# Layer 3 of a four-layer convolution chain: GpSimd's side work paced by an account of its own, and the next heads' keys and values fetched one block earlier

## The chip, the cores and the metric

The kernel runs on one core of one Trainium2 chip. The metric is the device time of one execution in microseconds (us), lower is better; before the change it is 3645.99 us, the median of three runs (3644.94 to 3652.72). The core has five engines that matter here, each working through its own queue in order: TensorE (PE, with weight loads shown as PEld), VectorE (DVE), ScalarE (ACT), GpSimd (POOL) and SyncE (SP), which here issues nearly all DMAs.

## The reference, cut to what matters

Four layers follow each other, each `x = x + layer(groupnorm(x))` on `x` of shape (4, 256, 48, 48). Layers 0 to 2 are convolutions, and the change does not touch them. Layer 3 is an attention with box windows of three sizes (48, 24 and 12 rows and columns) and 8 heads of 32 channels:

```python
q, k = sigmoid(Wq x), sigmoid(Wk x)              # per head: 32 channels x 48 x 48
v = v / max(norm(v), 1e-12)
for w in (1, 2, 4):                              # window of 48/w x 48/w positions
    wk, wkv = box(k), box(k v^T)                 # sums over the window around each position
    attn = (q . wkv) / (q . wk + 1e-6)           # numerator / "norm"
out = Wout concat(attn of the 3 windows) + bout
```

## The kernel before, in words

**The stream.** The kernel does not build `k v^T` images. For each block it computes scores `s = k^T q` between 128 key positions and 384 query positions, multiplies them by 0/1 window masks into tiles `sm`, and multiplies `sm` by `v` into three accumulators `acc`, one for each window. A block is (batch b, half of the heads ct, band of 8 rows rb): 4 x 2 x 6 = 48 blocks, numbered 0 to 47 in this order. A block has 12 to 18 steps, one for each tile of 8 x 16 key positions; the list `stream` (L2106) has 720 steps in all. The loop at L2143 does, for step n: the scores of step n on TensorE, the masks of step n, and then the sums (`acc`) of step n - 2 (`LAG = 2`). VectorE and ScalarE take the masks out of PSUM; GpSimd makes the mask of the narrowest window from an `sm` tile that VectorE or ScalarE has written (`masked`, L1809). In the trace these are the POOL operations `sm<-sm,masks`. So TensorE needs GpSimd's product of step n just before its scores of step n + 3.

**Everything else is put between the steps.** All instructions keep the order in which the Python code issues them (class `InOrder`; this is why nearly every line of the profile reads L147, and why groups are told apart by their tiles). Side work is written as generators, "jobs", and `advance()` (L241) lets each job issue its next piece after every step. The jobs are

- the projections of the next batch to q, k, v (`Projection`, L425: `sq`, the squares of v, on GpSimd; a VectorE sum and a ScalarE root follow);
- `k_sums` (L1559): running sums of k down the image, eight GpSimd additions on `pt` for each band, in two portions of four, then a store to `kb_d`;
- `norms` (L1601): loads `nhi`, `nlo`, `nq`, up to twelve GpSimd operations on `nhi` in four portions of three, a TensorE product, and the reciprocal by way of DRAM (`n_d`, `r_d`);
- `state` and `window_state` (L1700, L1730): for the part of the widest window in which every query sees every key, products of keys and values, then small GpSimd additions `kv` and `wide`;
- `prepare` (L1957): loads the first half's results `o` and the reciprocals `rc`, and multiplies them on GpSimd, three operations;
- `finish` (L1990): the output projection `out_ps`, two chains of six products.

**The account of TensorE.** `advance(time)` gives `spare`, the room that TensorE is expected to have in this step; a job that wants TensorE waits in `turn` (L268) or `bank` (L275) until `spare` is at least 0.6 of its cost, and takes the cost off. There is no account of GpSimd: a portion goes out at the step at which its job gets there.

**Forced steps.** Where the stream cannot go on without a job's result, `until(...)` (L257) calls `advance()` with unlimited room again and again, with no step of the stream in between. It is called for `("done", i - 2)`, since the sums of block i reuse the buffers of block i - 2, for `("window", i)` before the wide part of block i, and for q, k and v before they are loaded.

**Keys and values** of the next half of the heads are loaded by `load_kv` (L1686) at the end of the blocks that the table `LOADS` (L2059) names by their band, and each load starts a `state` job.

Of the kernel before, what the change touches and what calls it, by code (L numbers as in the profile page):

```python
# [22 lines left out]
B, C, H, W = 4, 256, 48, 48  # L23
# [3 lines left out]
RB = 8  # L27
NRB = H // RB
NB = RB * W
# [45 lines left out]
HEADS, D = 8, 32  # L75
# [75 lines left out]
def conv_preact_kernel(  # L151
# [82 lines left out]

    step, bank_free, spare = 0, 0, 0.0
    made = set()
    active = []

    def advance(time=None):  # L241

        nonlocal step, spare
        step += 1
        spare = ALL if time is None else min(spare, 0.0) + time
        for entry in list(active):
            if entry[0] <= step:
                wait = next(entry[1], None)
                if wait is None:
                    active.remove(entry)  # L250
                else:
                    entry[0] = step + wait
# [10 lines left out]
        while not made.issuperset(keys):  # L263
            yield 1

    ALL = 1e6

    def turn(cost):  # L268

        nonlocal spare  # L270
        while spare < 0.6 * cost:
            yield 1
        spare -= cost

# [22 lines left out]
    def take(what):  # L297
        while free[what] == 0:
            yield 1
        free[what] -= 1  # L300
# [11 lines left out]
    class Projection:  # L312
# [84 lines left out]
        def v(self, g, a, c):  # L397
            b = self.b
            while g not in self.xn or (c > 0 and g not in self.vs):
                if g in self.left:  # L400
                    return
                yield 1
            if c == 0:
                yield from take("vt")
                self.vs[g] = (
                    self.scr.tile([P, NKC, HEADS, D], F32, tag="vt", name="vt"),
                    self.scr.tile([P, NKC, HEADS], F32, tag="ss", name="ss"),
                )
            vt, ss = self.vs[g]
            yield from bank(1, NCT * product_time(C))  # L410
            ps = self.ps_tile()[:, 0:C].rearrange("p (h d) -> p h d", d=D)
            for ct in range(NCT):
                pe.matmul(
                    ps,
                    self.xn[g][:, ct, c, :],
                    proj["v"][:, ct, :],
                    start=(ct == 0),
                    stop=(ct == NCT - 1),
                )
            self.used(g)  # L420
            yield 1
            act.copy(vt[:, c], ps)
            yield 1
            yield from take("sq")
            sq = self.scr.tile([P, HEADS, D], F32, tag="sq", name="sq")  # L425
            pool.tensor_mul(sq, vt[:, c], vt[:, c])
            yield 2
            dve.tensor_reduce(ss[:, c, :], sq, AX.X, ALU.add)
            free["sq"] += 1
            if c < NKC - 1:  # L430
                return

            n = NKC * HEADS
            t = ss.rearrange("p k h -> p (k h)")
            r, s, u = (small.tile([P, n], F32, tag=f"{x}{n}", name=x) for x in ("vr", "vs", "vu"))
            dve.tensor_scalar_max(t, t, 1e-24)
            yield 1
            act.activation(s, t, AF.Sqrt)
            yield 1
            dve.reciprocal(r, s)  # L440
            dve.tensor_mul(u, t, r)
            dve.tensor_mul(u, u, r)
            dve.tensor_scalar(u, u, -0.5, 1.5, ALU.mult, ALU.add)
            dve.tensor_mul(r, r, u)
            dve.tensor_mul(
                vt,
                vt,
                r.rearrange("p (k h) -> p k h", h=HEADS)
                .unsqueeze(3)
                .to_broadcast([P, NKC, HEADS, D]),  # L450
            )
            yield 1
            sync.dma_start(out=v_d[b][:, a * NKC : (a + 1) * NKC], in_=vt)
            free["vt"] += 1
            made.add(("v", b, a))
# [1051 lines left out]
    with (  # L1507
# [51 lines left out]
        def k_sums(b, a, mo):  # L1559

            yield from wait_for(("k", b, mo, a))
            kp = kps[mo]
            chans = slice(mo * P, (mo + 1) * P)
            sync.dma_start(
                out=shifted(kp, 0),
                in_=kf_d[b][chans, a * NB : (a + 1) * NB].rearrange("p (r x) -> p r x", x=W),
            )
            yield FETCH
            yield from take("cs")
            cs = scr.tile([P, (RB + 1) * ROW], F32, tag="cs", name="cs", bufs=1)  # L1570
            n = GAP + RB * ROW
            for i, j in ((0, n // 2), (n // 2, n)):
                dve.tensor_tensor_scan(
                    cs[:, i:j],
                    kp[:, i:j],
                    kp[:, 0:1].to_broadcast([P, j - i]),
                    cs[:, i - 1 : i] if i > 0 else 0.0,
                    ALU.add,
                    ALU.add,
                )  # L1580
                yield 1
            pt = scr.tile([P, NW, RB, W], F32, tag="pt", name="pt")
            for wi, h in enumerate(HALVES):
                dve.tensor_sub(pt[:, wi], shifted(cs, h - 1), shifted(cs, -h - 1))
                yield 1
            free["cs"] += 1
            for r in range(RB):
                if a > 0 or r > 0:
                    up = pt[:, :, r - 1, :] if r > 0 else carry[:, mo]
                    pool.tensor_add(pt[:, :, r, :], pt[:, :, r, :], up)  # L1590
                if r == RB // 2 - 1:
                    yield 1
            pool.tensor_copy(carry[:, mo], pt[:, :, RB - 1, :])
            yield 1
            sync.dma_start(
                out=kb_d[b][:, chans, a * RB : (a + 1) * RB, :].rearrange("w p r x -> p w (r x)"),
                in_=pt.rearrange("p w r x -> p w (r x)"),
            )
            made.add(("kb", b, mo, a))

        def norms(b, rb):  # L1601
# [41 lines left out]
            for hi, lo, qf in loaded:  # L1643
                for wi, h in enumerate(HALVES):
                    n = min(RB, max(0, h + 1 - rb * RB))
                    if n < RB:
                        pool.tensor_sub(hi[:, wi, n:RB], hi[:, wi, n:RB], lo[:, wi, n:RB])
                yield 1
                for wi in range(NW):
                    pool.tensor_mul(hi[:, wi], hi[:, wi], qf)  # L1650
                sums.append(hi)
                yield 1
            yield 1
            yield from bank(HOLD, 2 * product_time(NB))
            ps = ps_m.tile([P, 512], F32, tag="st", name="norm_ps")
# [74 lines left out]
        def window_state(i):  # L1730


            b, ct, rb = order[i]
            rows = [a for a in range(NRB) if rows_whole(a, rb)]
            yield from wait_for(*(("state", b, ct, a) for a in rows))
            st = states[b, ct]
            t = scr.tile([P, NKC, D], F32, tag="kv", name="kv")
            pool.tensor_add(t, st[:, rows[0]], st[:, rows[1]])
            for a in rows[2:-1]:
                pool.tensor_add(t, t, st[:, a])  # L1740
            yield 1
            for g in range(HG):
                head = slice(g * D, (g + 1) * D)
                pool.tensor_add(wides[i % 2][head, :, head], t[head], st[head, rows[-1]])
            made.add(("window", i))
# [193 lines left out]
        def seen(wi, a, rb):  # L1939
            r0, r1 = rows_seen(wi, a, rb)  # L1940
            return r0 < r1
# [15 lines left out]
        def prepare(i):  # L1957
# [24 lines left out]

            yield FETCH
            for wi in range(NW):
                pool.tensor_mul(o[:, wi], o[:, wi], rcs[0][:, wi])
                yield 2
            free["rc"] += 1
            prepared[i] = o, res, rcs[1]

# [66 lines left out]
            load_kv(0, 0, a)  # L2056


        LOADS = {2: (0,), 3: (1, 2), 4: (3, 4), 5: (5,)}  # L2059
        finishing = []  # L2060

        def finish_all():
# [48 lines left out]
        def mask_time(i, a, c):  # L2111
# [11 lines left out]
                return time + product(1, cols_seen(1, c))  # L2123
            return time + 300

        def sums_time(i, a, c, at):

            rb, time = order[i][2], 0
            for wi in range(NW):
                if seen(wi, a, rb):  # L2130
                    y0, y1 = rows_seen(wi, a, rb)
                    parts = strips(c) if wi == 0 and rows_whole(a, rb) else [cols_seen(wi, c)]
                    time += product_time((y1 - y0) * sum(p1 - p0 for p0, p1 in parts))
            if at == 0:
                time += 300
            if at == 6:
                time += product_time(sum(RB * (c1 - c0) for c0, c1 in map(cols_whole, range(NKC))))
            return time
# [4 lines left out]
        for n in range(len(stream) + LAG):  # L2143
# [8 lines left out]
            if n >= LAG:  # L2152
# [11 lines left out]
                        blocks[i].sums(wi, a, c, sms)  # L2164
                if last:
                    done(i)
            time = 1000.0
            if LAG <= n < len(stream):
                time = 150.0 + mask_time(*stream[n][:3]) - sums_time(*stream[n - LAG][:4])
            advance(max(time, 150.0))  # L2170
        while active:
            advance()

# [43 lines left out]
```

## Time and profile before

| | |
|---|---|
| median of three runs | 3645.99 us (3644.94 to 3652.72) |
| the profiled execution, its own time | 3656.03 us |
| its span in the trace | 3654.3 us |
| layers 0 to 2, up to the first scores | 1396 us |
| layer 3's stream, to the end | 2258 us |
| TensorE busy in the stream | 2015 us |
| GpSimd busy in the stream | 1513 us |
| VectorE, ScalarE busy in the stream | 1484 us, 401 us |

The profile page slices the span in 40 equal parts of 91 us; the stream is roughly parts 16 to 40. A row of waits names the waiting engine and tile, the one that ended the wait, the sum in us, how often, and the longest. A line of the timeline has the start in us, the duration, engine and line, the operation with its tiles and how many were merged, and in brackets the idle time of the engine just before and what ended it.

### The profile page before, as it was taken

The numbers are of one execution on the slowest core, as the hardware profiler recorded it, in microseconds if no ns is written. First come the engines' busy times: TensorE is split into PE (matmuls) and PEld (weight loads), VectorE is DVE, ScalarE is ACT, GpSimd is POOL, SyncE is SP. The second block draws the span as 40 slices with busy tenths as digits, with TensorE's granted clock in tenths as the row PEclk, the third lists the DMA queues.
The fourth block names the chain that finished last, engine by engine and source line by source line (L and its number), as shares of the span: only waits on it lengthen the run. The fifth ranks groups of instructions, "written<-read, shape, count | busy, mean of one in ns | idle before, by whom it ended". The sixth has DMA issues, their size and how long they took to land. (4 is left out here: it accounts for less than half of the span.)

```text
span 3654.3 us, 73033 instructions
## 1 busy us (share of the span) xinstructions
PE 3184.0 (87%) x28754; PEld 1921.4 (53%) x28754; DVE 2408.1 (66%) x4987; ACT 677.1 (19%) x1557; POOL 1668.1 (46%) x2548
## 2 busy tenths in 40 slices
PE   3589998998998787888889888899898999899998
PEld 2467686786776564444444444444444444444444
DVE  7876587488474356687756567766567766566665
ACT  0012111111213522221101132211123211111110
POOL 0000020030030125697876577877557876555554
PEclk9789999999999898999889999999999999999999
DMA  7746324323313513353634343434323434311221
GB/s 251 228 140 189 114 82 129 109 91 116 124 51 119 164 68 97 103 156 121 180 98 121 98 137 123 127 124 143 87 72 121 147 111 137 84 40 37 69 70 51
DMA packets 373031, 422.76 MB, mean 116 GB/s; under 512 B 129075, under 2 KB 328531, under 8 KB 371667
## 3 DMA queue, kind: packets, MB, share of 16 engines
q1 hardware_dynamic: 371491, 416.32, 36.7%
q8 instruction: 229, 3.75, 0.4%
q0 software_dynamic: 144, 0.99, 0.1%
q14 instruction: 111, 0.91, 0.1%
q10 hardware_dynamic: 1056, 0.79, 0.1%
HBM read 287.74 MB, written 131.25 MB: 115 GB/s over the span
## 5 line engine op out<-in xcount | busy, mean ns | idle before, releaser
L147 DVE TENSOR_TENSOR sm<-s,masks 128x128 f32<-128x128 f32 (+8 forms) x2592 | 1146.4, 496 | 716.9 <-PE s L147 305.6
L147 POOL TENSOR_TENSOR sm<-sm,masks 128x432 f32<-128x432 f32 (+14 forms) x1152 | 824.1, 728 | 688.7 <-DVE sm L147 513.6
L147 PE MATMUL s<-qs,ks 32*128 32x320 f32 (+3 forms) x5760 | 819.4, 511 | 109.0 <-DVE sm L147 55.8
L147 PE MATMUL acc<-sm,vs 128*32 128x64 f32 (+13 forms) x14976 | 689.9, 310 | 49.0 <-POOL sm L147 48.2
L147 PE MATMUL cv<-vx,wt 128*128 128x288 f32 x2080 | 562.5, 427 | 93.1 <-DVE vx L147 50.7
L147 PEld LDWEIGHTS acc<-sm,vs 128*32 128x32 f32 x14976 | 354.2, 112 | 466.2 <-issue 273.0
L147 PEld LDWEIGHTS s<-qs,ks 32*128 32x128 f32 x5760 | 329.5, 190 | 487.7 <-issue 204.5
L147 PEld LDWEIGHTS cv<-vx,wt 128*128 128x128 f32 x2080 | 404.3, 199 | 215.3 <-issue 55.1
L147 POOL MEMSET v<- 128x16 f32 (+1 forms) x120 | 18.5, 215 | 727.8 <-DVE vx L147 633.6
L147 ACT COPY sm<-s 128x234 f32<-128x234 f32 (+5 forms) x384 | 124.5, 342 | 868.1 <-PE s L147 720.5
L147 PE MATMUL cv<-v,wl 128*128 128x384 f32 x1152 | 225.2, 356 | 24.3 <-DVE x L147 9.1
L147 PEld LDWEIGHTS cv<-v,wl 128*128 128x128 f32 x1152 | 215.7, 196 | 33.9 <-issue 15.8
L147 POOL TENSOR_TENSOR pt<-pt 128x144 f32<-128x144 f32 x336 | 189.8, 565 | 23.8 <-DVE pt L147 1.0
L147 POOL TENSOR_TENSOR v<-l2v,v 128x384 fp32r<-128x384 f32 x96 | 108.9, 1163 | 130.2 <-ACT v L147 121.5
L147 POOL TENSOR_TENSOR nhi<-nhi,nq 128x384 f32<-128x384 f32 x144 | 144.7, 1032 | 0.1
L147 PE MATMUL cv<-pad,wl 128*128 128x384 bf16 x864 | 143.1, 328 | 0.0
L147 PE MATMUL out_ps<-o,wout_sb 128*128 128x384 f32 x288 | 134.1, 548 | 4.2 <-DVE res L147 3.4
L147 ACT COPY stage<-acc 128x384 f32<-128x384 f32 x144 | 64.0, 488 | 365.3 <-PE acc L147 345.6
L147 PE MATMUL out_ps<-stage,wout_sb 128*128 128x384 f32 x288 | 120.4, 501 | 0.0
L147 PE MATMUL proj_ps<-xn,wk_sb 128*128 128x384 f32 x192 | 89.8, 596 | 31.3 <-ACT sg L147 24.6
L147 DVE TENSOR_TENSOR vx<-v 128x868 f32<-128x868 f32 x112 | 115.3, 1055 | 0.5
L147 PEld LDWEIGHTS <-wl 128*128 128x128 bf16 x864 | 83.9, 97 | 59.4 <-issue 0.8
(174 smaller groups left out, 3320.0 us busy)
## 6 DMA issues: line engine op xcount, KB each, us to landing
wt<-wt SPq DMA_DIRECT2D x48, 768.0 KB
kb_d<-pt SPq DMA_DIRECT2D x48, 576.0 KB
rc<-r_d SPq DMA_DIRECT2D x192, 144.0 KB
nhi<-kb_d SPq DMA_DIRECT2D x120, 192.0 KB
nlo<-kb_d SPq DMA_DIRECT2D x88, 192.0 KB
o_d<-stage SPq DMA_DIRECT2D x24, 576.0 KB
o<-o_d SPq DMA_DIRECT2D x24, 576.0 KB
wl<-wl_d SPq DMA_DIRECT2D x16, 768.0 KB
```

The source lines that it names most:

```text
L147: return lambda *args, **kwargs: self.tc.keep_in_program_order(op(*args, **kwargs))
```

## The change

GpSimd gets an account like TensorE's. `advance` gives `slack` as well, 1000 ns and the expected time of the step's masks less GpSimd's own mask time; `pool_turn` holds a job back until `slack` is at least 0.3 of the cost of its next GpSimd operations, and takes the cost off. Marked `urgent`, it only takes the cost off. `k_sums` now goes by two additions at a time, `norms` and `prepare` by one operation at a time, and the fixed pauses between their portions go. TensorE's threshold in `turn` becomes 0.3 too, and that of `bank` stays 0.6. Every entry of `LOADS` moves to the band before.

```diff
-    def advance(time=None):
+    def advance(time=ALL, pool_time=ALL):
         step += 1
-        spare = ALL if time is None else min(spare, 0.0) + time
+        spare = min(spare, 0.0) + time
+        slack = min(slack, 0.0) + pool_time
...
+    def pool_turn(elements, times=1, urgent=False):
+        nonlocal slack
+        cost = times * pool_op(elements)
+        while slack < 0.3 * cost and not urgent:
+            yield 1
+        slack -= cost
+
+    def pool_op(elements):
+        return 190 + 1.95 * elements
+
     def turn(cost):
-        while spare < 0.6 * cost:
+        while spare < 0.3 * cost:
...
             yield from take("sq")
+            yield from pool_turn(C, urgent=True)
...
             for r in range(RB):                                   # k_sums
+                if r % 2 == 0:
+                    if r > 0:
+                        yield 1
+                    yield from pool_turn(NW * W, 2)
                 if a > 0 or r > 0:
                     up = pt[:, :, r - 1, :] if r > 0 else carry[:, mo]
                     pool.tensor_add(pt[:, :, r, :], pt[:, :, r, :], up)
-                if r == RB // 2 - 1:
-                    yield 1
...
                     if n < RB:                                    # norms
+                        yield from pool_turn((RB - n) * W)
                         pool.tensor_sub(hi[:, wi, n:RB], hi[:, wi, n:RB], lo[:, wi, n:RB])
-                yield 1
-                for wi in range(NW):
+                    yield from pool_turn(NB)
                     pool.tensor_mul(hi[:, wi], hi[:, wi], qf)
                 sums.append(hi)
-                yield 1
...
+            yield from pool_turn(NKC * D, 2, urgent=True)         # window_state
             t = scr.tile([P, NKC, D], F32, tag="kv", name="kv")
...
-            yield 1
             for g in range(HG):
+                if g % 2 == 0:
+                    yield 1
+                    yield from pool_turn(NKC * D, 2, urgent=True)
...
             for wi in range(NW):                                  # prepare
+                yield from pool_turn(NB)
                 pool.tensor_mul(o[:, wi], o[:, wi], rcs[0][:, wi])
-                yield 2
+                yield 1
...
-        LOADS = {2: (0,), 3: (1, 2), 4: (3, 4), 5: (5,)}
+        LOADS = {1: (0,), 2: (1, 2), 3: (3, 4), 4: (5,)}
...
+        def far_time(i, a, c):
+            rb = order[i][2]
+            wi = NW - 1 if seen(NW - 1, a, rb) else 1
+            if not seen(wi, a, rb):
+                return 0
+            (y0, y1), (x0, x1) = rows_seen(wi, a, rb), cols_seen(wi, c)
+            return 2 * pool_op(2 * (y1 - y0) * (x1 - x0))
...
-            time = 1000.0
+            time, pool_time = 1000.0, 1000.0
             if LAG <= n < len(stream):
-                time = 150.0 + mask_time(*stream[n][:3]) - sums_time(*stream[n - LAG][:4])
-            advance(max(time, 150.0))
+                masks_ = mask_time(*stream[n][:3])
+                time = 150.0 + masks_ - sums_time(*stream[n - LAG][:4])
+                pool_time = 1000.0 + masks_ - far_time(*stream[n][:3])
+            advance(max(time, 150.0), max(pool_time, 150.0))
```

More of the change, by code (lines that the diff above doesn't have):

```diff
@@ L232, in conv_preact_kernel @@
     proj = {}
-    step, bank_free, spare = 0, 0, 0.0
+    ALL = 1e6
+    step, bank_free, spare, slack = 0, 0, 0.0, 0.0
     made = set()
     active = []
-    def advance(time=None):
-        nonlocal step, spare
+    def advance(time=ALL, pool_time=ALL):
+        nonlocal step, spare, slack
         step += 1
-        spare = ALL if time is None else min(spare, 0.0) + time
+        spare = min(spare, 0.0) + time
+        slack = min(slack, 0.0) + pool_time
         for entry in list(active):
@@ L264, in wait_for @@
             yield 1
-    ALL = 1e6
+    def pool_turn(elements, times=1, urgent=False):
[6 more added lines that the diff above has]
+        return 190 + 1.95 * elements
     def turn(cost):
         nonlocal spare
-        while spare < 0.6 * cost:
+        while spare < 0.3 * cost:
             yield 1
```

## The prediction

> **What bounds the kernel now.** I read the page's slices first, for where GpSimd is loaded, then busy time by stretches of the stream (the columns are stretch, length, then busy us and count of PE, PEld, DVE, ACT and POOL, then clock, DMA share and GB/s), then TensorE's waits from 1396 us on.
>
> ```profile
> POOL 0000020030030125697876577877557876555554
> 1721.00:2010.00 289.00, 257.09 (x2858) 122.92 (x2856) 188.82 (x399) 34.74 (x102) 220.77 (x317) 0.93 0.46 133
> 3393.00:3654.30 261.30, 242.13 (x2825) 118.48 (x2825) 160.00 (x354) 26.54 (x78) 130.58 (x193) 0.99 0.22 66
> PE acc L147 <- POOL sm L147: 48.2, 44, 4.9
> PE acc L147 <- POOL wide L147: 14.2, 3, 7.1
> PE norm_ps L147 <- ACT sg L147: 9.0, 1, 9.0
> ```
>
> TensorE is busy for 2015 of the stream's 2258 us, so its gaps, 243 us, are all that a new order of the same instructions can save. The last stretch, with almost no side work, has 19 us of gaps in 261; the second has 32 in 289, with GpSimd at 76%. TensorE waits 62.4 us on GpSimd itself. The timeline shows how:
>
> ```profile
> 1820.30 3.21 POOL L147 TENSOR_TENSOR nhi<-nhi,nq 128x384 f32<-128x384 f32 x3
> 1823.47 1.79 POOL L147 TENSOR_TENSOR sm<-sm,masks 128x312 f32<-128x312 f32 x2
> 1824.59 0.46 PE L147 MATMUL acc<-sm,vs 128*32 128x156 f32 x4 [2.90 <-POOL sm L147]
> ```
>
> Three `nhi` stand in GpSimd's queue ahead of a mask, the mask is late, and the sums wait 2.90 us. The lateness also goes round by other queues:
>
> ```profile
> 1697.86 2.62 POOL L147 TENSOR_TENSOR pt<-pt 128x144 f32<-128x144 f32 x4
> 1700.51 0.37 SPq L147 DMA_DIRECT2D kb_d<-pt  x1
> 1701.81 1.35 SPq L147 DMA_DIRECT2D q_d<-sg  x2
> 1705.68 1.28 ACT L147 ACT_TABLE_LOAD   x1 [7.49 <-DMA q_d<-sg]
> 1707.52 1.50 PE L147 MATMUL norm_ps<-nhi,head_sel 128*32 128x384 f32 x6 [8.97 <-ACT sg L147]
> ```
>
> `pt` is late, SP's store of it holds back the stores of `sg` behind it, ScalarE waits for those to reuse the buffer, and TensorE waits 8.97 us for ScalarE.
>
> **What the Trainium skill says.** "Perfetto Trace Analysis", Optimization Strategy, says to look for the gaps of the contended engine and for the semaphore that ends each; that is the method here, and its warning in Identifying the Most-Contended Engine that matmul busy time hides pipelining is why I count gaps and not the 89%. "GPSIMD Engine Reference", Elementwise, gives about 2.6 cycles an element at 1.2 GHz for two inputs, an estimate of 832 ns for 384 elements ahead of dispatch; the page's row for `nhi` has 1032 ns, and I use that. "DMA: Bandwidth & Descriptors", Anatomy of one DMA, says that a semaphore is waited for on the issuing sequencer before dispatch; the 1700.51 and 1701.81 lines agree.
>
> **Part 1, the bursts that go.** No instruction is added or removed on any engine; only the order changes. I counted in the built order what side work each step puts into GpSimd's queue, at the page's means (`pt` 565 ns, `nhi` 1032 ns; `o` 1011, `sq` 652 from the groups). Before, 30 of 720 steps put in over 4 us, against a mean step of 3.1 us; after, 11, and ten of these are forced stretches. So the paced part does what it says. Its account has room: the formula allows 299 us per batch, the side work is about 250. The TensorE waits for `sm` in blocks whose bursts are broken up sum, from the timeline, to 33.4 us: blocks 3 and 4 1.7, block 5 2.4, 7 5.8, 8 8.2, 15 5.5, 17 to 19 6.0, 30 and 31 3.8. I take three quarters, 25 us, because the account forgets unspent room and new small clusters appear (steps 457 to 462). The roundabout wait, 9.0 us, goes too. If the smoothed queue were still late by the same amount, this part would be worth nothing.
>
> **Part 2, `LOADS` one band earlier.** Both forced stretches on windows 24 and 36 (steps 368 and 548) go from the order, with one wait each:
>
> ```profile
> 3181.26 2.18 PE L147 MATMUL acc<-qs,wide 128*128 128x192 f32 x5 [3.58 <-POOL wide L147]
> ```
>
> That is 7.2 us. The third `wide` wait, 7.1 us at step 8, stays: it is the first block's. The earlier loads are part of the same 96 DMAs, a block sooner in SP's queue; the buffers hold two halves, so no load waits for one, and no stretch is forced on k or v.
>
> **Part 3, a load that leaves ScalarE's way.** At step 182 ScalarE waited for a batch-1 input queued on SP behind a dozen norm loads, with TensorE behind it:
>
> ```profile
> 2032.24 1.30 ACT L147 ACTIVATE xn<-xr,st 128x384 f32<-128x384 f32 x2 [14.44 <-DMA xr<-x_d]
> 2033.97 1.70 PE L147 MATMUL s<-qs,ks 32*128 32x320 f32 x8 [6.80 <-ACT sm L147]
> ```
>
> After, those loads are issued earlier and `xn` comes outside the stretch: 6.8 us gained. The four items make 25 + 9.0 + 7.2 + 6.8 = 48 us.
>
> **Part 4, the forced stretches, which grow.** Pacing delays `k_sums`, these delay `norms`, `norms` delays `prepare` and `finish`; so finished blocks are asked for too early more often. After the first block the order has 33 forced advances before and 50 after: new stretches at steps 137 (eight), 350 and 530 (five each), longer ones at 170 and 299. In a forced advance the room is unlimited, so `pool_turn` never yields and the twelve `nhi` that were four portions come out as one. What a burst costs is seen at step 542:
>
> ```profile
> 3153.39 2.93 POOL L147 TENSOR_TENSOR nhi<-nhi,nlo 128x384 f32<-128x384 f32 x3
> 3166.77 1.76 POOL L147 TENSOR_TENSOR sm<-sm,masks 128x168 f32<-128x168 f32 x3
> 3167.34 0.96 PE L147 MATMUL acc<-sm,vs 128*32 128x84 f32 x10 [4.85 <-POOL sm L147]
> ```
>
> Its scores end at 3151.07. The burst of twelve `nhi` and two `o` delays the mask to 15.7 us after that. TensorE is covered for 11.4 us, by three pairs of `out_ps` (1.3 us each), the sums in hand and three steps; the rest is the wait. I price each stretch so. At 350 and 530 the norm loads are issued inside the stretch, and GpSimd waits for them in its queue. At step 182 before, such a wait ended 6.6 us after the end of the scores (2017.19):
>
> ```profile
> 2016.98 0.33 SPq L147 DMA_DIRECT2D r_d<-nr  x1
> 2023.83 1.01 POOL L147 TENSOR_TENSOR nhi<-nhi,nlo 128x384 f32<-128x384 f32 x1 [4.14 <-DMA nlo<-kb_d]
> ```
>
> So 6.6 + 13.4 of work (3153.39 to 3166.77 above) = 20.0, less 11.4 of cover: 8.6 us each, 17.2. At 137: eight `pt` and `carry` fill the time until the loads land at 7.5, then twelve `nhi`, three `o`, four `pt` to 24.7; five pairs of `out_ps` cover 15: 9.7, less the 2.6 us that block 9 loses now, 7.1. At 299: ten `nhi`, three `o`, cover 10: 4.2. At 362 and 542 a third `o` and the single burst make 5.9 each, against 1.7 and 4.85 now: 5.3. At 182: 2.9. At 170 and 194: 1.4 against 5.4 now, a gain of 4.0. The sum is 33 us lost. Not seen in any trace of before is a stretch with sixteen loads and 22 us of side work at once; from below it costs 0 (loads landed, cover as long as the burst), from above 20 us at 137 and 18 at each of 350 and 530 (no cover but `out_ps`), 30 us more than I take.
>
> **Part 5, edits costed at nothing.** `turn` at 0.3 lets a chain's later products start in tighter steps; TensorE's work is the same, and the cover is that it is the busy engine anyway; if two products then crowd one step, VectorE idles for one product, about 1.3 us. `bank`'s threshold is unchanged, and so are the 40 us of waits of `proj_ps` on ScalarE's `sg` and `vt`, within 10 us either way. Four of the last block's products move from the tail into the last steps, where gaps are small: 0 to 1 us.
>
> **Sum.** 3656.0 - 48 + 33 = 3641 against the profiled execution's own time. That execution lies 10 us above the median, so the forecast for the median is **3631 us**, 0.4% faster. A measurement of this kernel can tell about 0.2%, 7 us, from no change.
>
> **Rivals.** *Forced stretches decide* (0.23, slower): the mechanism is the single burst of Part 4, its place steps 137, 350 and 530, its price up to 18 to 20 us each. Against the gain of 48 it decides once the stretches cost over 55 us together; at 33 + 30, with half of the 25 us, it gives 3646 + 63 - 35 = 3674. For it speaks that these stretches are new and carry more than any before; against it, that the 14 us burst at 542 cost just 4.85. *The smoothing is hidden anyway* (0.17, no change): TensorE's waits for GpSimd turn into waits on VectorE's or ScalarE's masks, which already sum to 102 us, so that only Parts 2 and 3 remain; with half of Part 4's loss that is about 3648. *More follows than I count* (0.10): smoother `sq` and `pt` also shorten the `proj_ps` waits, by half of 40 us, and the loads in the stretches land early: 3600. That the change does not do what it says is excluded by the order for GpSimd, except in forced stretches.
>
> **From cases to numbers.** The likeliest case (0.5) has 3631, its own range 3617 to 3645. The range of 3602 to 3664 reaches into the slower and the better case and leaves out about 2 in 10. Faster by over 0.2%: 0.43 from the first case, 0.10 from the last, 0.01 else: 0.54. Within: 0.07 + 0.14 + 0.02 = 0.23. Slower: 0.23.
>
> **What would show it.** Right: TensorE's wait for `wide` falls from 14.2 to 7 us; the 9 us of `norm_ps` on `sg` and the 6.8 us near step 182 are gone; no wait for `sm` over 2 us in blocks 5 to 8; new ones of about 9 us after steps 137, 350 and 530, behind a run of twelve `nhi`. Wrong: waits for `sm` as large as 48 us outside forced stretches, or over 15 us behind each of the three.

## The result, and the profile after

The changed kernel takes 3653.54 us (median of 22 runs, 3639.23 to 3668.93), against 3652.01 us (22 runs, 3640.86 to 3660.14) for the kernel before on the same chips. The ratio is 1.001, with a 95% interval of 0.9998 to 1.0021: no change that can be measured. The forecast had been 0.4% faster. Single runs scatter (standard deviation 6 to 7 us), so the experiments are read by their ratios to the kernel before, whose intervals are narrower, and "us under the changed kernel" below is the difference of two such ratios times 3652; such a difference is uncertain by 6 to 11 us.

The page of the changed kernel shows the same shape of GpSimd's load as before:

```profile
POOL 0000030030030124688986577776556687645554
```

The first slices of the stream are a little lower (`4688986` where `5697876` stood), the later ones are hardly different. So the account spreads the load over a few steps, not over a batch. Two stretches, with the columns of the prediction's windows:

```profile
1690.00:1981.00 291.00, 253.38 (x2866) 123.67 (x2865) 203.01 (x417) 35.06 (x103) 236.52 (x342) 0.95 0.45 131
3392.00:3648.80 256.80, 239.66 (x2820) 117.55 (x2816) 158.54 (x356) 24.57 (x69) 131.67 (x193) 1.00 0.23 67
```

In the quiet last stretch TensorE's gaps are 17 us of 257 (19 of 261 before). In the busy one, where the change was to help, they are 38 of 291, against 32 of 289. TensorE's waits from the first scores (1391 us) on, the largest rows:

```profile
PE s L147 <- DVE sm L147: 63.2, 151, 3.5
PE s L147 <- ACT sm L147: 50.7, 94, 5.9
PE proj_ps L147 <- ACT sg L147: 47.0, 22, 5.7
PE acc L147 <- POOL sm L147: 27.9, 15, 6.0
PE proj_ps L147 <- ACT vt L147: 19.6, 21, 1.7
PE out_ps L147 <- DVE res L147: 9.7, 5, 2.5
PE acc L147 <- POOL wide L147: 6.1, 1, 6.1
```

The sums wait for GpSimd's `sm` 15 times instead of 44, and for 27.9 us instead of 48.2; `wide` falls from three waits to one; the 9 us wait of `norm_ps` is gone. What the prediction counted on did happen. But the projections, `proj_ps`, now wait 66.6 us for ScalarE's `sg` and `vt`, and waited 39.7 before. The rows of the kernel before:

```profile
PE s L147 <- DVE sm L147: 55.8, 153, 2.9
PE s L147 <- ACT sm L147: 46.0, 90, 6.8
PE proj_ps L147 <- ACT sg L147: 29.0, 18, 4.3
PE proj_ps L147 <- ACT vt L147: 10.7, 12, 1.8
```

The two traces, and three of the experiments told below, side by side (worked out from each trace, from the first scores to the end; "at half clock" is busy time under a record of the granted clock of 0.50; "evacuations" are `sg`, `vt`, `ns`, `keys` and `state`; the 4 to 5 us after TensorE's last product are in neither busy time nor gaps):

| us | before | after | e3 | e14 | e11 |
|---|---|---|---|---|---|
| stream | 2258.4 | 2257.8 | 2188.3 | 2207.4 | 2177.6 |
| TensorE busy | 2015.6 | 2007.4 | 1984.6 | 1995.3 | 1986.7 |
| - of it at half clock | 184.5 | 172.3 | 117.6 | 142.7 | 127.9 |
| gaps | 238.6 | 246.1 | 199.4 | 207.8 | 185.9 |
| - waits on GpSimd | 62.5 | 35.9 | 10.8 | 30.8 | 18.7 |
| - on ScalarE's evacuations | 60.3 | 76.4 | 50.6 | 41.6 | 55.5 |
| - on VectorE's masks | 55.8 | 63.2 | 60.6 | 55.4 | 66.6 |
| - on ScalarE's masks | 46.0 | 50.7 | 45.3 | 53.2 | 33.8 |
| - on VectorE's `res`, `stage` | 5.0 | 12.4 | 25.4 | 19.5 | 4.4 |

From before to after, 26.6 us of waits on GpSimd go, and 16.1 (evacuations), 7.4 and 4.7 (masks) and 7.4 (`res`, `stage`) come. So the gaps grow by 7.5 us, and the busy time falls by 8.2. Where that came from is what the experiments are about. Some matmul records can be missing from a trace, so differences of a few us in one row carry nothing.

### The profile page after: what moved, and what is told of

Same layout as the page of the kernel before. It is cut to its first block, busy times and chain, and to the rows that moved or that the text cites. A ratio compares the mean times of both kernels' runs of the same rounds, so it can differ in the third digit from the quotient of the medians.

```text
span 3648.8 us, 73056 instructions
## 1 busy us (share of the span) xinstructions
PE 3170.3 (87%) x28754; PEld 1919.7 (53%) x28754; DVE 2410.3 (66%) x4987; ACT 677.7 (19%) x1557; POOL 1667.4 (46%) x2548
## 5 line engine op out<-in xcount | busy, mean ns | idle before, releaser
L147 PE MATMUL s<-qs,ks 32*128 32x320 f32 (+3 forms) x5760 | 824.9, 510 | 120.8 <-DVE sm L147 63.2
L147 PE MATMUL acc<-sm,vs 128*32 128x64 f32 (+13 forms) x14976 | 679.7, 309 | 28.3 <-POOL sm L147 27.9
L147 PEld LDWEIGHTS cv<-vx,wt 128*128 128x128 f32 x2080 | 402.7, 198 | 214.6 <-issue 55.4
```

Source lines behind the costliest of these rows:

```text
L147: return lambda *args, **kwargs: self.tc.keep_in_program_order(op(*args, **kwargs))
```

## The experiments

### The two halves of the change

e1 is the kernel before with the new table of loads; e2 is the changed kernel with the old one.

```diff
-        LOADS = {2: (0,), 3: (1, 2), 4: (3, 4), 5: (5,)}     # e1, on the kernel before
+        LOADS = {1: (0,), 2: (1, 2), 3: (3, 4), 4: (5,)}
```

> The kernel before with the moved LOADS table alone. Theory A (the account's gain was real and was given back in forced stretches and on SP's queue): TensorE's wait for wide falls from 14.2 to about 7 us, time 5 to 7 us under before (ratio 0.998). Theory B (gaps behind GpSimd are hidden: other waits take their place one for one): wide falls as well, the time stays (1.000).

> The changed kernel with the LOADS table of before. The built order then has forced stretches of 15 and 13 advances on windows 12 and 36. Theory A: these add two waits of TensorE for wide of some 5 us each and bursts of 12 us of side work, so 5 to 12 us slower than the kernel before (1.002 to 1.003). Theory B: as before and after (1.000).

Measured: e1 0.9976 (0.996 to 0.9992), e2 0.9971 (0.9961 to 0.9982). Each half alone makes the kernel faster, by 9 and 11 us; together they give nothing. e2 had been expected slower and is not. Its order has the forced stretch at step 137 but none at 299 and 350, and stretches on windows 12 and 36 (steps 188 and 548) of 15 and 13 forced advances. So the account does not lose by itself. The halves differ from their union in which forced stretches there are, and the next experiment changes these.

### The forced stretches, with the account kept

In the changed kernel a forced advance has unlimited room, so every job, not only the one that is waited for, puts all the GpSimd work that it has ready into the queue. e3 keeps the account there, so that each forced advance brings about one operation.

```diff
     def until(*keys):
         while not made.issuperset(keys):
-            advance()
+            advance(pool_time=1000.0)
```

> The changed kernel in which a forced advance gives GpSimd's account 1000 ns instead of unlimited room, so that the twelve nhi no longer come out as one burst (largest side work of a step 10 us instead of 22). Theory A: TensorE's wait for sm falls from 27.9 to under 12 us, and the time by 10 to 18 us (ratio to before 0.996 to 0.998), less what the more numerous forced advances (85 against 60) take. Theory B: the wait falls, the time stays at 1.001.

Measured: 0.9822 (0.9803 to 0.984), 3591.38 us. That is 69 us under the changed kernel and far more than either theory had given. The stretches get more advances (85 in all, 60 after, 42 before) and carry less: the largest burst of side work after the first block is 10.2 us, where it was 22.5 at step 137. TensorE's waits of e3:

```profile
PE proj_ps L147 <- ACT sg L147: 22.3, 14, 4.4
PE proj_ps L147 <- ACT vt L147: 15.9, 17, 2.1
PE out_ps L147 <- DVE stage L147: 15.1, 11, 2.5
PE out_ps L147 <- DVE res L147: 10.3, 10, 2.5
PE acc L147 <- POOL wide L147: 4.5, 1, 4.5
PE acc L147 <- POOL sm L147: 4.4, 8, 2.3
```

`sm` has fallen from 27.9 to 4.4: most of this was the wait behind the stretches' own bursts. But `sg` has fallen too, from 47.0 to 22.3, and no stretch stands beside most of those waits. The stretches pay for the pacing with 13 us of waits on `stage` and `res`. And by the table TensorE's busy time is 22.8 us less for the same instructions: a third of the gain lies in no gap at all. The busy time at half clock is 54.7 us less (the last section comes back to this).

Which stretches is it? e9 keeps the account only in the stretches at steps 350 and 530. e14 keeps it only in those of blocks 7 to 11 (steps 137 to 194), e15 only in those from block 18 on.

```diff
-            advance()
+            advance(pool_time=1000.0 if keys in ((("done", 21),), (("done", 33),)) else ALL)    # e9
+            advance(pool_time=1000.0 if keys[0][0] == "done" and keys[0][1] in
+                    (7, 8, 9, 10, 11) else ALL)               # e14; e15: 18 to 23, 30 to 35
```

> The changed kernel in which only the forced stretches on blocks 21 and 33 (steps 350 and 530) give GpSimd's account 1000 ns per advance; all others stay unlimited. The order then has one burst fewer at 350 and none at 530, while 362 grows to ten advances and keeps its burst. In the trace of after each of the two costs TensorE 6.9 us of waits. Price by gaps alone: 14 us under after (0.997 of before). With the clock as e8 showed (about 1.5 times the gap and more): 20 to 28 us under after (0.993 to 0.996).

> The changed kernel with GpSimd's account kept (1000 ns per advance) only in the forced stretches on blocks 7 to 11, at the turn from batch 0 to 1. The order then has no stretch left at 299 and 350, and the next batch's projections start 20 steps earlier (step 185 instead of 205). Theory D1 (the loss is lateness handed on: these stretches set how late everything after them is, and whether projections meet the norm loads): most of e3's 69 us, 40 us or more, and TensorE's waits on ScalarE's evacuation fall from 76 to about 55 us. Theory D2 (each stretch costs by itself, by its own burst): the bursts at 137, 170, 182, 194, 299 and 350 go, 18 us of gaps by the trace of after, so 18 to 30 us.

> The changed kernel with the account kept only in the forced stretches on blocks 18 and later; the first five stay as they are. The bursts at 299, 350, 362, 530 and 542 go, 31 us of gaps by the trace of after. D1: 10 to 25 us faster than after. D2: 31 to 50 us.

Measured: e9 0.9982 (0.9967 to 0.9996), 10 us under the changed kernel; e14 0.9893 (0.9876 to 0.991), 43 us under it; e15 0.9939 (0.9924 to 0.9955), 26 us under it. e14 came out as the first of its two theories had it, and e15 at the upper end of the first one's. 43 and 26 make the 69 of e3, but the two are not fully apart: with the account kept in the early stretches, the order of e14 has none at steps 299 and 350 either, and a new one at 155. The prediction had priced what e14 changes at 18.8 in all (7.1 + 2.9 - 4.0 for the early stretches, 4.2 + 8.6 for 299 and 350). By the traces e14 is 18 us ahead of the changed kernel at step 300, 32 at step 380 and 50 at step 480, so the gain goes on long after the stretches. Two rows of waits tell e14 and e15 apart, e14's first and then e15's:

```profile
PE acc L147 <- POOL sm L147: 22.6, 14, 6.1
PE proj_ps L147 <- ACT sg L147: 18.4, 14, 3.2
```

```profile
PE proj_ps L147 <- ACT sg L147: 37.9, 16, 5.8
PE acc L147 <- POOL sm L147: 8.2, 14, 2.3
```

Pacing the first stretches hardly moves the waits for `sm` (27.9 to 22.6); it takes away more than half of those for `sg`. Pacing the later ones does the opposite. So the early stretches cost more by what they move than by their own wait. Over steps 200 to 299, where most of the projections of batch 2 lie, the evacuation waits are 32.0 us in the changed kernel and 6.5 in e14. In the traces of e3 and e14 these projections begin at step 183; in the changed kernel they begin at step 203, and sixteen norm loads go out at steps 204 to 206. Lateness alone is not the reason: in the kernel before they begin later still, at step 209, as the last of its sixteen loads go out (206 to 209), and the waits over the same steps are 17.5 us. Why they are longer in the changed kernel than there was not taken apart.

e9 changes more than its two stretches as well. In its trace TensorE's waits at 350 and 530 fall from 16.3 to 5.2 us (steps 349 to 356 and 529 to 536), but those at 362 and 542 grow from 13.5 to 17.9 (steps 361 to 368 and 541 to 548), since the stretch at 362 now has ten advances and keeps its burst: 6.6 us less in all, for a gain of 10. With the uncertainty of such a difference, e9 does not tell whether a burst costs more than its wait.

### What a burst costs

The changed kernel's timeline at the forced stretch of step 350, SP's queue and TensorE's weight loads left out:

```profile
2545.07 0.91 PE L147 MATMUL out_ps<-o,wout_sb 128*128 128x384 f32 x2 [2.50 <-DVE res L147]
2546.26 0.99 POOL L147 TENSOR_TENSOR nhi<-nhi,nlo 128x384 f32<-128x384 f32 x1 [0.20 <-DMA nlo<-kb_d]
...
2551.19 0.82 PE L147 MATMUL s<-qs,ks 32*128 32x320 f32 x8
...
2557.50 0.99 POOL L147 TENSOR_TENSOR nhi<-nhi,nq 128x384 f32<-128x384 f32 x1
2558.45 1.94 POOL L147 TENSOR_TENSOR o<-o,rc 128x384 f32<-128x384 f32 x2
2560.35 1.97 POOL L147 TENSOR_TENSOR sm<-sm,masks 128x224 f32<-128x224 f32 x3
2561.02 1.38 PE L147 MATMUL acc<-sm,vs 128*32 128x112 f32 x14 [4.39 <-POOL sm L147]
```

GpSimd is busy without a break from 2546.26 to the mask at 2560.35, and TensorE waits 4.39 us for it, and 2.50 us before that for VectorE: 6.9 us, where 8.6 had been forecast. The windows after it, with the clock in the third column from the end:

```profile
2555.00:2561.00 6.00, 1.63 (x14) 0.63 (x8) 1.53 (x4) 0.58 (x2) 5.84 (x8) 0.97 0.37 122
2561.00:2567.80 6.80, 6.78 (x58) 3.00 (x58) 2.23 (x6) 0.47 (x1) 4.52 (x8) 0.53 0.36 96
2567.80:2575.00 7.20, 7.20 (x86) 3.77 (x86) 4.51 (x8) 0.00 (x0) 3.73 (x7) 1.00 0.02 3
```

For 6.8 us after the wait, TensorE is busy all the time and gets through 58 products; in the next 7.2 us, at clock 1.00, through 86. The wait is followed by a stretch at half clock, and no row of waits shows it. How much a burst costs in all was measured by itself. e8 is the kernel before, with six bursts of twelve products on a spare tile in batch 3, where GpSimd is least loaded:

```diff
+            if n in (571, 589, 607, 646, 661, 679):
+                for _ in range(12):
+                    pool.tensor_mul(extra, extra, extra)       # 128 x 384, reads and writes nothing else
```

> The kernel before with one burst of twelve extra 128x384 GpSimd multiplications (about 12 us, on a tile that nobody reads) after the masks of six steps (571, 589, 607, 646, 661, 679) of the last batch, where there is almost no side work; the computation stays whole. It prices one burst by itself. Price by gaps alone, as in the prediction: 12.4 + 1.3 of mask less about 8.5 of cover = 5 us each, 30 us in all (1.008). With the clock (records at 0.50 follow the larger waits): the same gaps, and 3 to 7 us more each from slower products, 48 to 72 us in all (1.013 to 1.020).

Measured: 1.0151 (1.0128 to 1.0175), 3705.7 us, 55 us or 9.2 us a burst (7.8 to 10.7). GpSimd and TensorE at the burst of step 571, then the windows around it:

```profile
3254.07 8.07 POOL L147 TENSOR_TENSOR extra<-extra 128x384 f32<-128x384 f32 x9
3262.10 1.12 POOL L147 TENSOR_TENSOR sm<-sm,masks 128x216 f32<-128x216 f32 x2
```

```profile
3262.73 1.54 PE L147 MATMUL acc<-sm,vs 128*32 128x108 f32 x16 [5.83 <-POOL sm L147]
3264.21 1.45 PE L147 MATMUL s<-qs,ks 32*128 32x320 f32 x8
```

```profile
3237.00:3257.00 20.00, 18.89 (x269) 9.46 (x266) 13.17 (x34) 3.14 (x10) 14.33 (x19) 0.98 0.19 61
3258.10:3268.30 10.20, 5.57 (x34) 3.28 (x38) 1.81 (x4) 0.00 (x0) 9.48 (x18) 0.50 0.01 2
3268.30:3285.00 16.70, 15.49 (x238) 7.88 (x232) 10.64 (x22) 1.09 (x4) 7.69 (x14) 1.00 0.01 2
```

The wait itself is 5.83 us (5.2 to 6.5 over the six; worked out by the prediction's rule it would be 5). The clock is at 0.50 for 10.2 us there, and for 6.8 to 10.2 us at each of the six; it falls 0.5 to 5.1 us after the wait began and comes back 3.1 to 5.8 us after its end. Eight products of scores take 1.45 us in it; eight of the same shape took 0.82 us at 2551.19 above. By the traces, from step 560 to the end this kernel takes 44.5 us more than the kernel before (480.1 against 435.6): 34.3 more in gaps and 10.2 more in busy time, so 5.7 and 1.7 a burst. That is 7.4 a burst, just under the interval of the timed runs; the two profiled executions lie only 44.6 us apart (3700.67 and 3656.03), and single executions scatter by as much as is missing. So a burst costs 7 to 9 us, more than its wait.

e4 asks how much there is to gain on GpSimd at all: it is the kernel before with most of the side work left out, so it is no version to use.

```diff
-                        pool.tensor_sub(hi[:, wi, n:RB], hi[:, wi, n:RB], lo[:, wi, n:RB])
+                        pool.tensor_sub(hi[:, wi, n:n + 1], hi[:, wi, n:n + 1], lo[:, wi, n:n + 1])
-                    pool.tensor_mul(hi[:, wi], hi[:, wi], qf)  # for each wi; and no additions on pt
+                pool.tensor_mul(hi[:, 0, 0:1], hi[:, 0, 0:1], qf[:, 0:1])
```

> The kernel before without most of GpSimd's side work: the running additions of pt are left out, and of the twelve nhi operations of a band and half only one row each is computed for the differences and one row of one window for the product (the norms are not computed). Loads, stores and all other engines' work stay. About 430 us of GpSimd's 1513 go. This bounds what any placing of that work can give. Theory A: TensorE's waits for GpSimd nearly vanish (under 10 us) and with them the indirect ones: 50 to 75 us faster (0.980 to 0.986). Theory B: under 25 us faster (0.993 or above).

Measured: 0.9679 (0.966 to 0.9698), 3536.49 us: by the ratio 117 us less, where both theories had put much less. The stream is 2140.6 us; gaps fall from 238.6 to 172.4 and TensorE's busy time from 2015.6 to 1963.9. So GpSimd's side work costs almost twice the 62.4 us of waits that name GpSimd. It does not do so by slowing the masks of other engines: VectorE's `sm` operations sum to 1285.7 us in the kernel before and 1288.0 in e4, ScalarE's to 131.5 and 131.7. e3's 1984.6 us of busy time is three fifths of the way there with all of the work done.

### ScalarE's and SP's queues

The longest wait of `proj_ps` for `sg` shows a wait that goes round by SP's queue. At step 206 of the changed kernel:

```profile
2067.80 0.32 SPq L147 DMA_DIRECT2D nhi<-kb_d  x1
2068.34 0.32 SPq L147 DMA_DIRECT2D nlo<-kb_d  x1
2068.89 0.79 SPq L147 DMA_DIRECT2D q_d<-sg  x2
2072.66 0.49 ACT L147 ACTIVATE sg<-proj_ps 128x384 f32<-128x384 f32 x1 [9.43 <-DMA q_d<-sg]
2073.20 1.65 PE L147 MATMUL proj_ps<-xn,wk_sb 128*128 128x384 f32 x2 [5.66 <-ACT sg L147]
```

The store of `sg` stands in SP's queue behind the norm loads; ScalarE has no free `sg` until it lands, and TensorE no free `proj_ps`. That is the roundabout wait that the change had taken away at 1707, in another place. Four buffers for `sg` should take it away, in the changed kernel (e5), in e3 (e6), and in the kernel before as a control (e13):

```diff
-            t = self.scr.tile([P, NB], F32, tag="sg", name="sg")
+            t = self.scr.tile([P, NB], F32, tag="sg", name="sg", bufs=4)
```

> The changed kernel with four buffers for sg (the tile into which ScalarE evacuates a projection) instead of two. The trace of after shows ScalarE waiting 9.43 and 7.80 us for the stores of sg, which stand on SP's queue behind the norm loads that the pacing has delayed into the next batch's projections. Theory A1 (that queue is where part of the gain went): TensorE's waits of proj_ps and keys_ps on ScalarE's sg fall from 52 us by 12 to 20, and the time by 10 to 25 us against after (ratio to before 0.994 to 0.998). Theory A2 (the waits come from ScalarE's own order, table loads and masks ahead of the evacuation): they fall by under 5 us, the time stays within 0.2% of after.

> The kernel before with four buffers for sg instead of two: the control to e5, which gained 0.6% on the changed kernel. If the waits behind SP's queue are new with the change: only the one wait of 9.0 us of norm_ps on sg can go here, and the time falls by 5 to 14 us (0.996 to 0.999). If the queue cost as much before: 20 us and more (0.9945 or below).

> Paced forced advances (as in e3) and four buffers for sg together. A1: another 5 to 15 us under e3 (0.978 to 0.981). A2: the same as e3 (0.982).

Measured: e5 0.9949 (0.9937 to 0.9962), 22 us under the changed kernel; e13 0.9944 (0.9928 to 0.9961), 20 us under the kernel before; e6 0.9808 (0.9789 to 0.9827), not to be told from e3. The kernel before gains as much as the changed one, so most of this price was there before the change. In the traces the stream alone becomes 19.5 us shorter in e5 and 9.7 in e13, and the first scores come 8 us earlier in both; that leaves room for some 10 us that the change brought, which single traces cannot settle. With paced stretches there is next to nothing left to gain; why was not taken apart. And e5's row is still high:

```profile
PE proj_ps L147 <- ACT sg L147: 34.2, 19, 4.6
```

A wait of another kind is seen at step 214 of the changed kernel, where ScalarE changes its table twice for one root, and `proj_ps` waits behind it; e5's longest, 4.6 us, is of about this size:

```profile
2103.25 1.28 ACT L147 ACT_TABLE_LOAD   x1
2104.54 0.22 ACT L147 ACTIVATE vs<-ss 128x24 f32<-128x24 f32 x1
2104.78 1.28 ACT L147 ACT_TABLE_LOAD   x1
2106.62 1.65 PE L147 MATMUL proj_ps<-xn,wk_sb 128*128 128x384 f32 x2 [4.57 <-ACT sg L147]
```

### The other edits

e7 is e3 with the old table of loads, e10 is the changed kernel with `turn` at 0.6 again.

> Paced forced advances (as in e3) with the LOADS table of before. The account with the old table (e2) was 0.4% faster than with the new one. Theory C1 (the new table hurts by itself under the account, its state products take the PSUM bank from norms and output projections): with the old table 5 to 15 us faster than e3 (0.978 to 0.981). Theory C2 (it hurt through which forced stretches fell where, and their bursts): once forced advances are paced the two tables are within 0.2% (0.980 to 0.984).

> The changed kernel with TensorE's threshold in turn back at 0.6 of the cost: the part costed at nothing, undone. The built order has the same forced stretches. If it is worth nothing: within 0.2% of after (0.999 to 1.003 of before). If crowded steps were part of what was lost: 5 us or more faster than after.

Measured: e7 0.9895 (0.9873 to 0.9917), e10 1.0015 (1.0 to 1.0029). The old table costs e3 27 us, though it had gained 14 in the unpaced kernel (e2). Neither expectation of e7 had that: under the account the earlier loads are a gain once the stretches are paced, and a loss while they are not. `turn` moves nothing, as the prediction had it.

### A faster version

e11 is e6 with more room in ordinary steps, e16 with more again, to see whether it is the room or the spreading that counts.

```diff
-                pool_time = 1000.0 + masks_ - far_time(*stream[n][:3])
+                pool_time = 1700.0 + masks_ - far_time(*stream[n][:3])      # e11; e16: 2500.0
```

> Paced forced advances and four buffers for sg (as e6), and 1700 instead of 1000 ns of base room per step in GpSimd's account, so that the side work is delayed less: 39 forced advances instead of 85, largest side work of a later step 7.2 us. Theory A (delay of the side work costs through forced stretches and projections that meet norm loads): 5 to 20 us faster than e6 (0.975 to 0.979). Rival (spreading matters, delay does not): GpSimd's masks are late more often, 5 to 15 us slower than e6 (0.982 to 0.985).

> As e11 with 2500 instead of 1700 ns of base room per step, close to no pacing outside forced stretches. If earlier side work is what counts: the same as e11 or up to 10 us faster (0.974 to 0.977). If spreading counts as well: 5 to 20 us slower than e11 (0.978 to 0.982).

Measured: e11 0.9765 (0.9742 to 0.9787), 3562.8 us; e16 0.9856 (0.984 to 0.9871), 3599.34 us. e11 is the fastest version that was run, 2.35% under the kernel before. With 1700 ns finished blocks are rarely asked for too early: 39 forced advances, where e3 has 85 and the kernel before 42. With 2500 ns 33 us of the gain are lost, with 41 forced advances in the built order; TensorE's waits on GpSimd are 37.7 us, where e11 has 18.7, and its busy time is 17.8 us longer. So the spreading counts too. e11's waits show both sides kept low:

```profile
PE s L147 <- ACT sm L147: 33.8, 86, 1.6
PE proj_ps L147 <- ACT sg L147: 26.5, 18, 4.4
PE acc L147 <- POOL sm L147: 11.9, 19, 2.0
```

## Why the prediction was wrong

**Parts 1 to 3 held.** Waits for `sm` outside forced stretches are nearly gone (the largest left are 2.29 us at step 126 and 1.0 at 197), the 8.97 us of `norm_ps` is gone, `wide` fell from 14.2 to 6.1, and the 6.80 us near step 182 is 2.9, which Part 4 had put back. The signs that the prediction named for "right" were seen, but for the 2.29 us in block 8 and the somewhat shorter waits at 350 and 530, and the time did not follow. (Part 1 has the side work at about 250 us a batch; the trace has some 180, which leaves its account more room.)

**Part 4: the waits were sized about right, one by one.** From the timeline, forecast and measured: step 350 8.6 and 6.9; step 530 8.6 and 6.7; step 299 4.2 and 4.8; steps 362 and 542 5.9 each and 5.9, 6.0; step 137 9.7 before what block 9 had lost, and 10.3 (2.89 for GpSimd's `sm`, 3.51 for VectorE's, 3.87 for `res` and `stage`). Neither bound, 0 or 18 to 20 each, came near.

**The step that failed** is in Part 5, among the edits costed at nothing: the waits of `proj_ps` on ScalarE's `sg` and `vt` were to stay as they are, "within 10 us either way", because `bank`'s threshold is unchanged. They rose by 27 us (39.7 to 66.6). By the prediction's sum TensorE's gaps were to shrink by 15 us; in the traces they grew by 7.5, and this one term is larger than the miss of 22.5. An unchanged threshold does not keep these waits as they were: they hang on ScalarE and, by way of the stores, on SP's queue (steps 206 and 214 above), and the change moves what stands there.

e14 ties the rise to the forced stretches: with the account kept in those of blocks 7 to 11, the waits of `proj_ps` on `sg` and `vt` are 31.5 us, less than before the change, and the kernel is 43 us faster. So Part 4, which priced each stretch by its own wait, left out more than it counted: it has the stretches lose 33 us against the kernel before, and e3 shows that the unlimited room in them costs 69. How the 43 us of e14 divide between SP's queue, ScalarE's table loads and what goes with the two stretches that disappear was not taken apart; in the traces 38 of 50 us are gaps, and 12 are busy time.

**A premise was wrong as well**, though it did not make this forecast miss: that TensorE's gaps, 243 us, are all that a new order can save. Busy time was held constant, and it is 2015.6, 2007.4 and 1984.6 us in before, after and e3, of which 184.5, 172.3 and 117.6 at half clock. From before to after this worked in favour of the change. It hides a good part of what was still to be had, 22.8 of e3's 69 us. A burst in a quiet stretch costs 7 to 9 us for a wait of 5.8 (e8); e9 is too close to tell.

**Part 5's other items held**: `turn` is worth nothing that can be measured (e10).

**The rivals.** "Forced stretches decide" had the right place: the stretches ate the gain, but did not pass it, so the time is not slower, and the waits at 137, 350 and 530 were 10.3, 6.9 and 6.7 us instead of 18 to 20; most of their cost lay elsewhere. "The smoothing is hidden anyway" had the right outcome, no change, mostly by luck: waits on VectorE's and ScalarE's masks did rise, but by 12 us, less than half of the 26.6 that went on GpSimd, and e4 and e3 show that the smoothing is far from hidden. "More follows than I count" is about what happens once the stretches are paced as well: in e14 the evacuation waits are 19 us under those of the kernel before.

**Not settled**: why e1 and e2 gain 9 and 11 us and their union none. e7 shows that the table's sign turns with the pacing of the stretches; through which stretch was not tried. Nor was a version in which only the job that is waited for has unlimited room.

## What to carry to other kernels

A pacing rule has to hold in the forced path too: where the stream stops for one job, unlimited room lets all the others use the stop to fill the queue. Then look for what the stop has moved, not only for its own wait. Price a wait of the busiest engine by more than its length when the page's clock falls with it, by putting a burst of known size into a quiet stretch and timing it. And when an order delays some work to smooth it, try several sizes of the room: too little, and the work is often asked for too early (85 forced advances with 1000 ns); too much, and the masks are late again (2500 ns); 1700 was the best of the three here (e11).

## What the runs showed of the hardware

At each of the six waits of 5.2 to 6.5 us in e8 the clock is at 0.50 for 6.8 to 10.2 us, of which the last 3.1 to 5.8 lie after the wait. The stretch of step 137 of the changed kernel has several such turns in a row:

```profile
1840.40:1847.20 6.80, 5.67 (x9) 3.20 (x10) 3.36 (x5) 0.00 (x0) 6.35 (x9) 0.50 1.02 286
1847.20:1857.50 10.30, 7.22 (x111) 3.59 (x109) 2.97 (x5) 1.07 (x3) 9.91 (x11) 1.00 1.03 321
1857.50:1867.70 10.20, 6.54 (x38) 2.72 (x38) 3.63 (x8) 1.05 (x3) 9.96 (x16) 0.50 0.35 101
1867.70:1878.00 10.30, 9.53 (x134) 5.05 (x130) 7.71 (x19) 1.14 (x4) 9.12 (x17) 1.00 0.20 67
```

The lengths, 6.8 and about 10.2 us, are two and three times 3.4 us. The Trainium skill, "TensorE: Matmul & The Clock Gate", Part 1: The HAM clock gate, says that the clock is either full or half, and that one idle window of about 3.4 us brings it to half. The records here agree with the two values (no trace of this case has a third) and with the length of the window. They show no sharp limit for the wait. In ten of the traces (before, after, e1, e2, e3, e5, e8, e11, e14 and e15), from 60 us after the first scores on, all 83 waits of 3.5 us or more that began at full clock had a record of 0.50 that began in them or within 3.5 us after; so had 52 of 70 waits of 2.0 to 2.5 us, and 35 of 150 of 1.0 to 1.5 us.

What it costs can be read from the products. In the kernel before, eight products of scores (32x320) take 1.45 us at half clock (median of 12 such groups) and 0.86 at full (397 groups), so an estimate of the time lost is 1 - 0.86/1.45, or 0.4, of the busy time at half clock. It fits: in all 17 traces TensorE's busy time less that share is between 1927 and 1950 us, while the busy time itself goes from 1964 to 2017. For the changed kernel it comes to 70 us of 172, about 1.9% of its time. The page's figure of under 1% of a typical kernel is for the ramp at the start; where the busiest engine waits often for a few us in mid-stream, the clock is a term of its own.
